# Two-layer sequence kernel: the feed-forward's first norms move in front of a branch, into a pool of their own

## The chip, the cores and the metric

One core of one Trainium2 chip. Its engines work side by side, each through its own list of instructions in order: TensorE (PE, with its weight loads PEld), VectorE (DVE), ScalarE (ACT), GpSimd (POOL), and SyncE (SP), which here only starts DMAs. The metric is the device time of one execution in microseconds, the median of several runs. Matrices are in 32-bit floats.

## The reference, cut to what matters

The kernel takes 4096 tokens of 256 features through two layers of two parts each, every part behind a layer norm and added back to its input:

```
x = x + attn0(norm(x))   # fast-weight memory with two decays
x = x + ffn0(norm(x))    # 8 experts, the best 2 of them for each token, hidden size 1024
x = x + attn1(norm(x))   # RWKV: time mix with a recurrence, then channel mix
x = x + ffn1(norm(x))    # five ternary weight matrices, three hidden layers of 1024
```

The change touches the last line's norm, and the order of work between the second, third and fourth line:

```
h = silu(x @ w1.T * s1) * (x @ w2.T * s2)
h = gelu(h @ h1.T * sh1);  h = gelu(h @ h2.T * sh2);  y = h @ w3.T * s3
```

## The kernel before

**Stages.** The first stage does attn0 and routes the tokens; its SBUF pools are then closed (`ctx_a.close()`, line 1240). What follows is in two blocks with a branch between them.

- In front of the branch, the experts of ffn0 run over slots of 256 tokens (`experts`, line 1307): 31 slots that are surely needed. attn1 works on chunks of 256 tokens (`mixing`, line 1466); chunk n needs only finished expert rows, so its steps are mixed in between the experts' steps. The same block checks the feed-forward's weights in 22 parts (`ff_check`, line 1261): a DMA brings a part into the one buffer `fft`, and three DVE instructions (`differences`: round, compare, reduce) count in `odd` whether any weight would change by rounding. `ff_flag` (line 1282) puts the 22 counts together with a transpose on PE.
- The branch (`other_slots`, line 1422; profile line 1425) tests on every engine whether a 32nd and further slots are in use. With these inputs none is: each engine takes the arm without work, where it only raises the semaphores that the other arm would have raised.
- Behind the branch, the rest of attn1 is mixed with ffn1 (`ff_split`, line 1912), which works on pairs of chunks. Each 512-token operand is split into a rounded part `hi` and a rest `lo`, so that each product is two matmuls with float32r operands. The weights come in 22 parts per pair, with DMAs that POOL starts (`fetch`, line 1978; the tile `part` has four buffers).

**The order** is written out by hand. A step is put into a `Plan` with a time and a rank, and `run` emits the steps in order of time, then rank, then entry. In the front block the unit is one step of an expert slot, 16 to a slot: for slot s, `up` at 16s to 16s+7, `down` (of a slot that isn't the last) at 16s+24 to 16s+31, the copy `xgT` (`keep`, line 1352) at 16s-7, the two `y` additions (`add`, line 1378) at 16s+28 and 16s+32, the `ys_d` store on POOL (line 1384) at 16s+32. Part q of the weight check is loaded at 12q and counted at 12q+9.5. attn1 has a time of its own, 22 units to a chunk (`TURN`, `WHEN`, line 1454): a step of chunk n is due at 22n plus its entry in `WHEN`, for example `sides` 32, `flip_c` and `keep_c` 54, the third `share` 33; the result of chunk n (from 1 on) is there at 22n+74. `among` (line 1301) turns such a time into a front time, from 208 on. All steps before `CUT` go into the front block, the others (`later`) behind the branch.

**The norm of ffn1** belongs to `pair`. For each chunk, `moments` (line 1940) takes mean and variance on DVE, `roots` (line 1948, through `root_of`, line 1440) adds epsilon on DVE and takes the power -0.5 on POOL, `norm` (line 1952) scales on DVE into `xf`, `flip` (line 1961) transposes on PE into `xfT`, and `keep` (line 1971) splits into `xf_p_hi` (ACT) and `xf_p_lo` (DVE). `first` (line 1997) is the first product, profile tile `pf`. For chunks 1 and 2, the first pair, the steps are due at 98 to 101.5 and 120 to 123.5, times before or about at the cut; being part of `ff_split` they come at the head of the block behind the branch.

**Memory.** Pools on the left side of SBUF are stacked: the weights and pools of attn1 (`rw`, `cc`, `c1`, `c2`), later `d2` of ff_split. The experts' pools (`me`, `mw`, `mt`) are on the right and are closed behind the branch (`moe_stack.close()`, line 2171). `d2` is then opened over the gap and over their bytes. A pool opened without an option waits as a whole: the first instruction of each engine that touches it waits for everything that was closed before. `mw` and `mt` have `reuse_waits="tile"`: there each tile waits only for what lay in its own bytes.

Of the kernel before, what the change touches and what calls it, by code (L numbers as in the profile page):

```python
# [8 lines left out]
F32 = mybir.dt.float32  # L9
# [3 lines left out]
ALU = mybir.AluOpType  # L13
AX = mybir.AxisListType

P = 128
S = 4096
D = 256
# [32 lines left out]
def mk_seq_kernel(ctx: ExitStack, tc: tile.TileContext, a: dict, out: bass.AP):  # L51
    nc = tc.nc
# [15 lines left out]
    ident = const.tile([P, P], F32, name="ident")  # L68
# [40 lines left out]
    for o, nm in ((0, "WkT"), (DS, "WqT"), (2 * DS, "WvT"), (3 * DS, "pwT")):  # L109
        n = a[nm].shape[1]  # L110
        nc.sync.dma_start(
            out=w_pj[:, :, o : o + n], in_=a[nm].rearrange("(c p) n -> p c n", p=P)
# [3 lines left out]
    for o, nm in ((0, "WvT"), (DS, "ir_w1T")):  # L116
        nc.sync.dma_start(
            out=w_vi[:, :, o : o + DS], in_=a[nm].rearrange("(c p) n -> p c n", p=P)
        )
    irb = ac.tile([P, 1], F32, name="irb")  # L120
    o, _ = _COLS["ir_b1"]
# [18 lines left out]
    def bcast(ap, shape):  # L140
        return ap.to_broadcast(shape)

    class Plan:
# [5 lines left out]
        def at(self, time, rank, step):  # L149
            self.steps.append((time, rank, len(self.steps), step))  # L150
# [7 lines left out]
    MIX, OUT, FEED, REST = range(4)  # L158
# [59 lines left out]
    with tc.tile_pool(name="pow", bufs=1) as tmp:  # L218
        shift1 = tmp.tile([P, P + 1], F32, name="shift1")
        nc.gpsimd.affine_select(  # L220
            out=shift1, in_=ones, pattern=[[1, P + 1]], compare_op=ALU.is_equal, fill=0.0,
# [31 lines left out]
        out=before, in_=ones[:, : NE * NE].rearrange("p (i j) -> p i j", i=NE),  # L253
# [7 lines left out]
    for q in range(2):  # L261
        t = ac.tile([P, NT, 4, DS], F32, name=f"kq{q}")
# [3 lines left out]
    for q in range(3):  # L266
        t = ac.tile([P, P], F32, name=f"h{q}")
# [12 lines left out]
    for r in range(2 * NE * S // (8 * P)):  # L280
        d, r = (xe_d, ys_d)[r * 8 * P // (NE * S)], r % (NE * S // (8 * P))
        nc.sync.dma_start(
            out=d[r * 8 * P : (r + 1) * 8 * P, :].rearrange("(p r) d -> p r d", r=8),
            in_=bcast(zero.unsqueeze(1), [P, 8, D]),
# [37 lines left out]
        out=earlier, in_=ones[:, :P], pattern=[[1, P]], compare_op=ALU.is_gt, fill=0.0,  # L322
# [20 lines left out]
    def moments(b, z, key, i):  # L343
        if i == 0:
            z["st"] = a2.tile([P, NT, 6], F32, tag=f"{key}_st", name=f"{key}_st_{b}")
            z["mv"] = a2.tile([P, NT, 2], F32, tag=f"{key}_mv", name=f"{key}_mv_{b}")
        nc.vector.bn_stats(out=z["st"][:, i, :], in_=X[b][:, i, :])
        nc.vector.bn_aggr(out=z["mv"][:, i, :], in_=z["st"][:, i, :])
# [838 lines left out]
    def table_end():  # L1187
# [28 lines left out]
    at = (  # L1216
        ((END - 25, END - 17), (END - 17, END - 5)), ((END - 5, END + 3), (END + 3, END + 12.5)),
        ((END + 13, END + 21), (END + 21, END + 29)), ((END + 29, END + 37), (END + 37, END + 45)),
    )
# [22 lines left out]
    ctx_r = ExitStack()  # L1242
# [18 lines left out]
    def ff_check(plan, time, q):  # L1261
        nm, src, j, kc, n = FFP[q]
        z = {}

        def load():
            z["t"] = mt.tile([P, kc, n], F32, tag="fft", name=f"fft_{q}", bufs=1)
            nc.sync.dma_start(
                out=z["t"], in_=a[src][j * P : (j + kc) * P, :].rearrange("(c p) n -> p c n", p=P)
            )

        def differences():
            r = mt.tile([P, kc, n], F32R, tag="ffr", name=f"ffr_{q}", bufs=1)
            nc.vector.tensor_copy(r, z["t"])
            nc.vector.tensor_tensor(z["t"], z["t"], r.bitcast(F32), ALU.not_equal)
            nc.vector.tensor_reduce(
                odd[:, q : q + 1], z["t"].rearrange("p c n -> p (c n)"), AX.X, ALU.max
            )

        for k, step in ((0, load), (9.5, differences)):
            plan.at(time + k, REST, step)  # L1280

    def ff_flag():
# [10 lines left out]


    SLOT = 2 * NF
    CUT = 120

    NSURE = 2 * S // SL + 3 - NFULL
    AMONG = ((0, 0.0), (6, 8.3), (7, 9.5), (8, 12.5), (12, 24.5), (22, 3.0 * SLOT))
# [108 lines left out]
    def first_slots():  # L1408
        plan = experts(range(NSURE), NSURE - 1)
        for k, (w, nm) in enumerate(((w_tm, "W_tm"), (w_cm, "W_cm"), (w_cp, "W_cp"))):  # L1410
            plan.at(
                40 + 20 * k, REST,
                lambda w=w, nm=nm: nc.sync.dma_start(
                    out=w, in_=a[nm].rearrange("(c p) n -> p c n", p=P)
                ),
            )
        for q in range(len(FFP)):
            ff_check(plan, 12 * q, q)
        plan.at(12 * len(FFP) + 4, REST, ff_flag)
        return plan  # L1420
# [14 lines left out]
    NI = TC // P  # L1435
# [4 lines left out]
    def root_of(rs, var):  # L1440
        nc.vector.tensor_scalar(rs, var, LN_EPS, None, ALU.add)
        nc.gpsimd.tensor_tensor(rs, rs, mhalf[:, 0, :], ALU.pow)
# [5 lines left out]
    def tokens(d, n):  # L1448
        return d[n * TC : (n + 1) * TC, :].rearrange("(i p) d -> p i d", p=P)
# [5 lines left out]
        load=2, gathers=(-2, -1, 0, 1), combine=12, moments=13, roots=13, norm_a=14, norm_i=14,  # L1455
# [453 lines left out]

    def ff_split(own, plan):

        d2 = own.enter_context(tc.tile_pool(name="d2", bufs=2))
        at = plan.at
        TP = 2 * TC
        banks = [0]
# [1 line left out]
        def psf(shape, name):  # L1919
            banks[0] += 1  # L1920
            if banks[0] % 4:
                return psa(shape, name)
            return ps.tile(shape, F32, tag="p", name=name, bufs=1)
# [12 lines left out]
        def pair(p, two, base):  # L1936

            z = {"part": {}}

            def moments(g):  # L1940
                n, x, _ = two[g]
                st = d2.tile([P, NI, 6], F32, tag="st", name=f"ln5_st_{n}", bufs=1)
                mv = z["mv"] = d2.tile([P, NI, 2], F32, tag="mv", name=f"ln5_mv_{n}", bufs=1)
                for i in range(NI):
                    nc.vector.bn_stats(out=st[:, i, :], in_=x()[:, i, :])
                    nc.vector.bn_aggr(out=mv[:, i, :], in_=st[:, i, :])

            def roots(g):
                z["rs"] = d2.tile([P, NI], F32, tag="rs", name=f"ln5_rs_{two[g][0]}", bufs=1)
                root_of(z["rs"], z["mv"][:, :, 1])  # L1950

            def norm(g):
                n, x, _ = two[g]
                z["xn"] = d2.tile([P, NI, D], F32, tag="xn", name=f"xf_{n}", bufs=1)
                for i in range(NI):
                    nc.vector.tensor_scalar(
                        z["xn"][:, i, :], x()[:, i, :], z["mv"][:, i, 0:1], z["rs"][:, i : i + 1],
                        ALU.subtract, ALU.mult,
                    )

            def flip(g):
                z["pt"] = psf([P, 2, TC], f"xfT_{two[g][0]}")
                for c in range(2):
                    for i in range(NI):
                        nc.tensor.transpose(  # L1965
                            z["pt"][:, c, i * P : (i + 1) * P],
                            z["xn"][:, i, c * P : (c + 1) * P], ident,
                        )

            def keep(g):  # L1970
# [93 lines left out]
                nc.sync.dma_start(out=tokens(out, two[g][0]), in_=z["ot", g])  # L2064

            for g in range(2):
                for t, rank, step in (
                    (1, REST, moments), (1, REST, roots), (2, REST, norm), (4.5, MIX, flip),
                    (4.5, REST, keep),
                ):  # L2070
                    at(two[g][2] + t, rank, lambda step=step, g=g: step(g))
                for t, rank, step in ((44, REST, again), (49, REST, store)):
                    at(base + t + 2 * g, rank, lambda step=step, g=g: step(g))
            for j in range(NF):
# [3 lines left out]
            for l, src in ((0, "h0"), (1, "sh1")):  # L2078
                t = base + 14 + 2 * NF * l
# [79 lines left out]

    front = Plan()  # L2160
    chunks = mixing(ctx_r, front)
    front.steps.sort(key=lambda s: s[:3])
    later = [s for s in front.steps if s[0] >= CUT]
    both = first_slots()
# [7 lines left out]
    with ExitStack() as own:  # L2172
        plan = Plan(later)
        pair = ff_split(own, plan)
        chunks = chunks[1:] + chunks[:1]
        for n, x, time in chunks:
            plan.at(time, REST, lambda n=n, x=x: nc.sync.dma_start(out=tokens(x2_d, n), in_=x()))
        for p in range(NC // 2):
            two = chunks[2 * p : 2 * p + 2]
            pair(p, two, two[1][2])  # L2180
        with tc.manual_schedule():
            plan.run()
# [92 lines left out]
```

## Time and profile before

| what | value |
|---|---|
| runs | 2042.1, 2046.39, 2045.76 us; median 2045.76 |
| the profiled execution | 2045.78 us |
| its span, first to last instruction | 2044.3 us |
| PE, PEld busy | 1951.9 us (95%), 1656.1 us (81%) |
| DVE, ACT, POOL busy | 1244.0 us (61%), 1016.1 us (50%), 437.8 us (21%) |
| mean granted TensorE clock | 0.983 |
| DMA | 314.86 MB, mean 154 GB/s |

How to read the lines: the profile follows one execution. Its row by slices cuts the span in 40 parts and gives the busy tenths of an engine in each. The chain of work is followed back from the last instruction to what released it, step by step. A row of the timeline has the start in us, the duration, engine, line, operation, the tiles written and read, the shape, a count, and in brackets how long the engine was idle before it and what ended that. A `q` behind an engine's name is its queue: branches and waits that aren't counted as busy. By stage, each column is one engine's busy us with its number of instructions; behind them stand the granted clock, the DMA share and GB/s.

### The profile page before, as it was taken

To read this page: it belongs to the slowest core of one execution; us is meant where nothing else is said; L and a number is where in the kernel's file an instruction comes from. 1 tells how busy PE (TensorE), PEld (TensorE's weight loads), DVE (VectorE), ACT (ScalarE), POOL (GpSimd) and SP (SyncE) were. 2 spreads that over 40 slices of the span, in tenths; PEclk is the share of its full clock that TensorE was granted. 3 is DMA by queue.
4 is the path that set the end of the run, shared out by engine and by line. 5 is a ranking of instruction groups with operands and counts; after the bars stand their busy time and mean duration, and the time that the engine had idled before them with its cause. 6 is when DMAs were issued, how large, how long until landed. Compare 5 with 4: busy or idle time off the path is not lost. (4 is left out here: it accounts for less than half of the span.)

```text
span 2044.3 us, 27834 instructions
## 1 busy us (share of the span) xinstructions
PE 1951.9 (95%) x9879; PEld 1656.1 (81%) x9879; DVE 1244.0 (61%) x3013; ACT 1016.1 (50%) x1918; POOL 437.8 (21%) x523
## 2 busy tenths in 40 slices
PE   6999999988899999999997999999999999999998
PEld 4888777777677888888886888888888888888887
DVE  4677888876333435564635768687676876754342
ACT  3665555433222223454534656577565675744342
POOL 1000222222300012121112223232323322122121
PEclk8999999988999999999998999999999999999999
DMA  9999300023477677554433555555565555555585
GB/s 316 342 343 343 110 32 32 32 84 102 168 260 266 227 252 249 178 178 150 147 124 84 109 118 119 114 135 103 113 135 103 134 111 118 109 114 119 102 179 105
DMA packets 328856, 314.86 MB, mean 154 GB/s; under 512 B 18177, under 2 KB 308609, under 8 KB 328705
## 3 DMA queue, kind: packets, MB, share of 16 engines
q1 hardware_dynamic: 158624, 187.61, 28.1%
q0 software_dynamic: 170080, 125.33, 27.9%
q8 instruction: 83, 1.36, 0.3%
q14 instruction: 69, 0.56, 0.1%
HBM read 215.64 MB, written 97.26 MB: 153 GB/s over the span
## 5 line engine op out<-in xcount | busy, mean ns | idle before, releaser
L1086 ACT ACTIVATE hT<-peh,b 128x256 f32<-128x256 f32 x248 | 115.6, 473 | 291.3 <-PE peh L1359 285.8
L1359 PE MATMUL peh<-xgT,w 128*128 128x256 f32 x992 | 229.2, 385 | 8.6 <-DVE y L1381 6.5
L1373 PE MATMUL peo<-w,hT 128*128 128x256 f32 x992 | 224.9, 379 | 0.0
L1359 PEld LDWEIGHTS peh<-xgT,w 128*128 128x128 f32 x992 | 189.2, 193 | 38.7 <-DVE y L1381 9.4
L1932 PE MATMUL psh<-h_hi,part 128*128 128x512 f32 x512 | 211.1, 412 | 0.0
L1932 PE MATMUL psh<-sh_hi,part 128*128 128x512 f32 x512 | 209.2, 409 | 0.0
L1373 PEld LDWEIGHTS peo<-w,hT 128*128 128x128 f32 x992 | 186.7, 190 | 24.4
L2045 DVE TENSOR_TENSOR sh_lo<-hf_sh,sh_hi 128x512 fp32r<-128x512 f32 x128 | 88.3, 690 | 186.3 <-ACT sh_hi L2044 186.3
L1932 PE MATMUL psh<-h_lo,part 128*128 128x512 f32 x512 | 200.5, 392 | 0.0
L1932 PE MATMUL psh<-sh_lo,part 128*128 128x512 f32 x512 | 200.2, 391 | 0.0
L2039 ACT ACTIVATE hf_sh<-psh,vec 128x512 f32<-128x512 f32 x128 | 87.8, 686 | 225.8 <-PE psh L1932 225.4
L619 PE MATMUL pf<-LY,LT 128*128 128x256 f32 x640 | 181.1, 386 | 3.4 <-DVE LY L645 2.2
L645 DVE TENSOR_TENSOR LY<-pf,LY 128x256 f32<-128x256 f32 x192 | 79.0, 417 | 77.4 <-ACT LY L641 50.2
L619 PEld LDWEIGHTS pf<-LY,LT 128*128 128x128 f32 x640 | 106.2, 191 | 22.2 <-issue 6.3
L1827 PE MATMUL pcm<-xcT,w_cm 128*128 128x256 f32 x512 | 120.9, 379 | 0.0
L1860 PE MATMUL pcp<-k,w_cp 128*128 128x256 f32 x512 | 120.9, 379 | 0.0
L612 ACT COPY LT<-pt 128x256 f32<-128x256 f32 x192 | 71.4, 372 | 87.7 <-PE pt L608 79.2
L1932 PEld LDWEIGHTS psh<-h_lo,part 128*128 128x128 f32 x512 | 96.3, 188 | 20.1 <-DVE h_lo L2045 0.4
L1932 PEld LDWEIGHTS psh<-sh_lo,part 128*128 128x128 f32 x512 | 96.3, 188 | 19.7
L1932 PEld LDWEIGHTS psh<-sh_hi,part 128*128 128x128 f32 x512 | 96.3, 188 | 19.5
L1932 PEld LDWEIGHTS psh<-h_hi,part 128*128 128x128 f32 x512 | 96.3, 188 | 19.4
L1860 PEld LDWEIGHTS pcp<-k,w_cp 128*128 128x128 f32 x512 | 97.0, 189 | 14.9
(421 smaller groups left out, 4186.4 us busy)
## 6 DMA issues: line engine op xcount, KB each, us to landing
w<-in_w_dram SPq DMA_DIRECT2D x62, 1024.0 KB
xe_d<-zero SPq DMA_DIRECT2D x32, 1024.0 KB
ys_d<-zero SPq DMA_DIRECT2D x32, 1024.0 KB
part<-in_h1T_dram POOLq DMA_DIRECT2D x64, 512.0 KB
part<-in_h2T_dram POOLq DMA_DIRECT2D x64, 512.0 KB
w_f<-in_w_dram SPq DMA_DIRECT2D x8, 1024.0 KB
part<-in_w1T_dram POOLq DMA_DIRECT2D x32, 256.0 KB
part<-in_w2T_dram POOLq DMA_DIRECT2D x32, 256.0 KB
```

The costliest lines, as they stand in the source:

```text
L612: nc.scalar.copy(y["LT"], y["pt"])
L619: nc.tensor.matmul(p[:, f].rearrange("p g t -> p (g t)"), LT[:, f, :], L[:, f].rearrange("p g t -> p (g t)"), start=True, stop=True,)
L645: nc.vector.tensor_tensor(N[:, :, 1, :], p[:, :, 1, :], L[:, :, 1, :], ALU.add)
L1086: nc.scalar.activation(out, x, AF.Gelu_apprx_tanh, bias=bias)
L1359: nc.tensor.matmul(z["ph", h], z["w1"][:, c, h * P : (h + 1) * P], z["xT"][:, c, :], start=(c == 0), stop=(c == 1),)
L1373: nc.tensor.matmul(z["px"], z["hT"][:, h, i * P : (i + 1) * P], z["w2"][:, h, :], start=(h == 0), stop=(h == NF - 1),)
L1827: nc.tensor.matmul(pk[:, u, :], w_cm[:, c, j * P : (j + 1) * P], z["xnT"][:, c, :], start=(c == 0), stop=(c == 1),)
L1860: nc.tensor.matmul(z["pv"][:, c, :], w_cp[:, j, c * P : (c + 1) * P], z["k2"][:, g, h, u, :], start=(half == 0 and q == 0), stop=(half == ...
L1932: nc.tensor.matmul(pp, w, x[u][:, k, :], start=(k == 0 and u == 0), stop=(k == kk - 1 and u == 1))
L2039: nc.scalar.activation(h, z[nm, j], AF.Gelu, scale=col(nm, j))
L2045: nc.vector.tensor_tensor(lo[:, j, :], h, hi[:, j, :].bitcast(F32), ALU.subtract)
```

## The change

Three things change.

1. `ff_norm`, a new function, does what `moments`, `roots` and `norm` did, with tiles from a new pool `cf` that is opened in front of the branch, on top of `c2`. The steps go into the front plan at the same times as before (`time` is 22n+75, and the steps lie 1, 1 and 2 behind it). `xf` has two buffers instead of one. `pair` now gets the normalized tile in place of the chunk, and its `flip` is due at the old time or at `CUT`, whichever is later.
2. `CUT` goes from 120 to 121.5. So the norms of chunks 1 and 2 (98, 99, 120, 121) are in front of the branch, and with them the steps of attn1 that are due from 120 up to 121.5: `flip_c` and `keep_c` of chunk 3, `sides` and the third `share` of chunk 4. `d2` gets `reuse_waits="tile"`.
3. `differences` of the weight check are due 11 units after their load instead of 9.5.

```
-        for k, step in ((0, load), (9.5, differences)):
+        for k, step in ((0, load), (11, differences)):
...
-    CUT = 120
+    CUT = 121.5
...
+    def ff_norm(cf, at, n, x, time):
+        z = {}
+        def moments():
+            st = cf.tile([P, NI, 6], F32, tag="st", name=f"ln5_st_{n}")
+            mv = z["mv"] = cf.tile([P, NI, 2], F32, tag="mv", name=f"ln5_mv_{n}")
+            for i in range(NI):
+                nc.vector.bn_stats(out=st[:, i, :], in_=x()[:, i, :])
+                nc.vector.bn_aggr(out=mv[:, i, :], in_=st[:, i, :])
+        def roots():
+            z["rs"] = cf.tile([P, NI], F32, tag="rs", name=f"ln5_rs_{n}")
+            root_of(z["rs"], z["mv"][:, :, 1])
+        def norm():
+            z["xn"] = cf.tile([P, NI, D], F32, tag="xn", name=f"xf_{n}", bufs=2)
+            for i in range(NI):
+                nc.vector.tensor_scalar(
+                    z["xn"][:, i, :], x()[:, i, :], z["mv"][:, i, 0:1], z["rs"][:, i : i + 1],
+                    ALU.subtract, ALU.mult,
+                )
+        for t, step in ((1, moments), (1, roots), (2, norm)):
+            at(time + t, REST, step)
+        return lambda: z["xn"]
...
-        d2 = own.enter_context(tc.tile_pool(name="d2", bufs=2))
+        d2 = own.enter_context(tc.tile_pool(name="d2", bufs=2, reuse_waits="tile"))
...
-                            z["xn"][:, i, c * P : (c + 1) * P], ident,
+                            two[g][1]()[:, i, c * P : (c + 1) * P], ident,
...
-                for t, rank, step in (
-                    (1, REST, moments), (1, REST, roots), (2, REST, norm), (4.5, MIX, flip),
-                    (4.5, REST, keep),
-                ):
-                    at(two[g][2] + t, rank, lambda step=step, g=g: step(g))
+                for rank, step in ((MIX, flip), (REST, keep)):
+                    at(max(two[g][2] + 4.5, CUT), rank, lambda step=step, g=g: step(g))
...
     chunks = mixing(ctx_r, front)
+    chunks = chunks[1:] + chunks[:1]
+    cf = ctx_r.enter_context(tc.tile_pool(name="cf", bufs=1))
+    chunks = [(n, x, time, ff_norm(cf, front.at, n, x, time)) for n, x, time in chunks]
...
-            two = chunks[2 * p : 2 * p + 2]
+            two = [(n, xn, time) for n, _, time, xn in chunks[2 * p : 2 * p + 2]]
```

The three inner functions `moments`, `roots` and `norm` of `pair` are removed with it.

More of the change, by code (lines that the diff above doesn't have):

```diff
@@ L1938, in pair @@
             z = {"part": {}}
[L1940 to L1959, printed above, removed]
             def flip(g):
@@ L2174, in mk_seq_kernel @@
         pair = ff_split(own, plan)
-        chunks = chunks[1:] + chunks[:1]
-        for n, x, time in chunks:
+        for n, x, time, _ in chunks:
             plan.at(time, REST, lambda n=n, x=x: nc.sync.dma_start(out=tokens(x2_d, n), in_=x()))
         for p in range(NC // 2):
-            two = chunks[2 * p : 2 * p + 2]
+            two = [(n, xn, time) for n, _, time, xn in chunks[2 * p : 2 * p + 2]]
             pair(p, two, two[1][2])
```

## The prediction

> **What bounds the kernel.** I read the page first. TensorE (PE) is busy 95% of the 2044.3 us span, and the row by slices has few dips:
>
> ```profile
> PE   6999999988899999999997999999999999999998
> ...
> PE 41%; ACT 3%; DVE 1%; another core or an unknown queue 0%; issue 0%; POOL 0%; DVEq 0%; POOLq 0%; ACTq 0%
> ```
>
> The chain that ended last is 41% PE and begins at 1086.65 us with a wait on something unnamed; from 1106 us to the end it is nearly all matmuls. So what shortens PE's idle time before 1106 us shortens the kernel. PE's idle by stage (columns: window, its length, then busy us of PE, its weight load, DVE, ACT, POOL, granted clock, DMA):
>
> ```profile
> 1040.00:1080.00 40.00, 39.97 (x192) 34.88 (x191) 13.05 (x32) 14.83 (x28) 3.42 (x5) 1.00 0.33 109
> 1080.00:1110.00 30.00, 18.65 (x81) 15.24 (x80) 14.69 (x40) 9.22 (x13) 9.21 (x13) 0.83 0.29 79
> 1110.00:1130.00 20.00, 20.00 (x95) 16.87 (x94) 18.15 (x31) 14.65 (x28) 7.54 (x8) 1.00 0.66 136
> ```
>
> PE is full on both sides of the branch and loses 11.4 us at it. The timeline there:
>
> ```profile
> 1085.76 0.42 DVE L1381 TENSOR_TENSOR y<-peo,b 128x256 f32<-128x256 f32 x1 [3.03 <-PE peo L1373]
> 1086.49 0.73 POOL L1384 DMA_DIRECT2D ys_d<-y  x1 [6.18 <-DVE y L1381]
> 1092.29 0.43 DVE L1945 BATCH_NORM_STATS2 ln_st<-xt 128x6 f32<-128x256 f32 x1 [6.10 <-DMA yg<-ys_d,placei]
> ...
> 1093.89 0.71 POOL L1442 TENSOR_TENSOR ln_rs<-ln_rs,mhalf 128x2 f32<-128x2 f32 x1 [6.68 <-DVE ln_rs L1441]
> 1094.57 0.73 POOL L1995 DMA_DIRECT2D part<-in_w1T_dram  x1
> ...
> 1095.26 1.09 PE L1965 MATMUL xfT<-ident,xf 128*128 128x128 f32 x4 [9.53 <-DVE xf L1956]
> ...
> 1106.37 0.50 PE L1932 MATMUL pf<-xf_p_lo,part 128*128 128x512 f32 x1 [1.80 <-DVE xf_p_lo L1975]
> ```
>
> PE's last expert matmul ends at 1085.72. Nothing runs until DVE's first norm at 1092.29; DVE, POOL, DVE, then PE follow in single file. What held DVE is shown by the branch's line:
>
> ```profile
> L1425 PEldq COMPARE_BRANCH x1: 3731/3731/3731, 1082.3 to 1082.3; - x1
> L1425 PEldq EVENT_SEMAPHORE  x1: 51/51/51, 1086.1 to 1086.1; - x1
> ...
> L1425 DVEq EVENT_SEMAPHORE  x1: 21/21/21, 1086.6 to 1086.6; - x1
> ...
> L1425 POOLq INC_SWDGE_SEM  x1: 1527/1527/1527, 1089.9 to 1089.9; - x1
> ```
>
> In the empty arm each engine raises its counters to what the untaken arms would have left. PE is through at 1086.16, DVE at 1086.65. POOL first waits for the last expert store (its semaphore completes at 1089.62), then raises the DMA counters, until 1091.43. DVE, ACT, PE and POOL each stand at nine waits on all these counters at the head of line 1945, 1974, 1965 or 1442, all in the first instruction that touches pool `d2`. At 0.1 us each these run from 1091.42 to 1092.29 on DVE.
>
> **Part 1, waits tile by tile.** Whether a tile of `d2` still waits for POOL's counters is decided by its bytes. In the compiled program of before, `c2` ends at byte 114,824 of a partition and `mt` begins at 137,952. The new pool takes about 4.2 KB of that gap, so `d2` starts near 119,070: the split tiles `xf_p_hi`/`lo` end near 127,270 and the first `part` buffer near 131,360. All lie in the gap, over first-stage memory released hundreds of us earlier. Tiles over `xg` and `y` (second `part` buffer, hidden layer) still wait for 1091.43, but POOL can't issue before that anyway and the hidden layer is written after 1097. I take the wait as gone for PE, ACT and DVE. PE's first transposes need DVE's arm (1086.65, the PSUM bank) and one 0.1 us step: start 1086.75 instead of 1095.26. Bounds: 1086.16 (PE's own arm) and 1092.35 (nine waits remain; rival 1).
>
> **Part 2, norms in front.** Per chunk: statistics, sum and scale 1.4 us DVE, 0.71 us POOL, 0.76 us DVE. They go before the branch. Cover: DVE is busy 13.05 of 40 us at 1040:1080 and idles 6.84 us before the last `xgT`; the power stands on POOL behind a store already issued (1052.46) and ahead of one that waits 12.6 us more. Cost there: nothing; without cover up to the round trip, 2.2 us per chunk. What else the new cut pulls in front: `sides` of chunk 4 (1.4 us DVE, same cover); `keep_c` and the last `share` (1.0 and 0.9 us ACT between gelus of 0.47 us each 0.86 us, three PSUM banks: nothing to 1.9 us; I take nothing, the gap of 0.39 per gelu being nearest); and `flip_c`, four transposes at 0.11 us steps on a full PE: **+0.44 us**. SP's next `xt` load (1095.42) no longer waits for a norm behind the branch and can't collide with the weights.
>
> **PE from 1086.75**, at full-clock steps (0.44 for four transposes, 1.73 for eight 256-wide matmuls): xfT 1087.2, pkvr 1088.9, pcm 1090.65, xfT 1091.1, pcm 1092.8. DVE meanwhile: lo at 1088.8, combine 1.65 to 1090.5, mix 0.87 to 1091.4, statistics and roots 1.43 to 1092.8, second lo 0.69 to 1093.5 (ACT's hi is done by 1092). Next late are the weights. POOL, without the powers, issues part 0 at 1091.5 and 1092.2; in before, three of the first four landed 3.2 to 3.5 us after issue (one 5.6, beside the `xt` load): 1094.9 and 1095.6. So the first 8 matmuls of `first(0)` (0.93 us per 4) run 1094.9 to 1096.75. In before the matmul after them began at 1108.09. **Gain 11.3 us.** DVE reaches the end of `xa` at 1096.65 (before 1109.35), in time for the transposes at 1098.5; after that PE is as full as at 1110:1130, so the shift stays.
>
> **Part 3, counts 1.5 units later.** DVE is in order, so a later time matters only where another DVE step lies in between. Expert steps lie at 9, 12 and 16 of each 16 units, the counts at 9.5, 5.5, 1.5, 13.5 and now at 11, 7, 3, 15: nothing between. Mixing steps begin at 208; only the last count (261.5 to 263) passes any: `maxima`, `mix(1)`, `steps` of chunk 0 (261.5, 262.9). There:
>
> ```profile
> 807.70 0.69 DVE L1273 CAST ffr<-fft 128x1024 fp32r<-128x1024 f32 x1 [5.91 <-DMA fft<-in_w3T_dram]
> ...
> 810.89 1.39 DVE L1655 TENSOR_TENSOR_SCAN m<-vec,carry_m,kvr 128x256 f32<-128x256 f32 x2
> ...
> 817.24 0.17 DVE L1283 TENSOR_REDUCE flag<-odd 128x1 f32<-128x22 f32 x1
> ```
>
> DVE idles 5.91 us for the last weights, then does `maxima`; PE waits 2.74 us for `flag` at 817.46. Reordered, `maxima` fits into the idle, `mix` runs when pkvr ends (808.1), the count from 810.2, flag near 816.0: **1.2 us less** (bounds 0 and 2.7).
>
> **Sum:** -11.3 + 0.44 - 1.2 = -12.1. The profiled execution took 2045.78 (span 2044.3 and 1.5 around it), the median of the runs is 2045.76: **2033.7 us**. Own range 2031.3 (flag's whole 2.7 saved, weights not waited for) to 2036.5 (weights 2.2 us later, as in the 5.6 us row; ACT 0.6).
>
> The clock: it was 0.5 for 10.24 us from 1089.13, after a 3.41 us window with PE idle. A window with PE 38% busy (543.00 to 546.41) was followed by 3.41 us at half, two at 60% (812.65 to 819.47) were not. My two pauses (1.0 and 2.1 us) leave 70% and, if the second falls into one window, about 40%: a drop of 3.41 us would cost 1.7, inside the range; I leave it out, since the phase of the windows is open. [...]
>
> **Rivals.**
>
> 1. *The waits stay* (a first tile still overlaps expert memory; the option doesn't do what it says). PE starts at 1092.35 at half clock until 1099.4: transposes 0.88, pkvr 3.46, pcm to 1099.8, the rest to 1101.9, next matmul at 1103.75: 4.35 saved, in all -5.1: 2040.7. For it: the arm's counters are still raised at 1091.4; against: the byte positions. 0.12.
>
> 2. *PE pays a second jump.* Its COMPARE_BRANCH took 3.73 us, hidden under matmuls until 1086.05. If the jump out of the arm costs as much, PE starts at 1089.9 behind an idle window, at half clock to about 1092.5; the matmul after `first(0)` begins near 1100: -8.9, 2036.9. Against: at the kernel's end PE took 3.35 us into the arm, but its next instruction followed the arm's wait within 0.2 us. 0.10. [...]
>
> 3. *Slower: late counts block DVE.* If a later count stood in front of an expert add, PE would stop as at 651.12, where DVE stood at a count for weights: 4.61 us idle and 3.41 us at half clock, 6.3 in all. Five counts stand just before an add; from two more such stops the 12.1 is gone, three give +6.8: 2052.6. Against: the order on DVE doesn't change there. 0.06.
>
> 4. *Gain given back* between 1097 and 1130, where DVE is 91% busy: within 4 us of now. 0.08.
>
> Forecast 0.64. Rival 1 lies just beyond the 0.2% (4.1 us) that a measurement of this kernel can tell from no change; I leave it with faster: 0.86 faster, 0.08 same, 0.06 slower. The range 2031.3 to 2040.9 holds forecast, rivals 1 and 2.
>
> **What would show it.** Right: PE's gap at the branch about 1 us, then at most 2 us before the first `pf`; no half clock there; `part` issued just after INC_SWDGE_SEM; `flag` gap near 1.5. Wrong: a `d2` tile in the tail of expert memory, PE starting after 1091, or new gaps before `peh` between 580 and 800.

## The result, and the profile after

| what | before | after |
|---|---|---|
| median of six runs each, same chip | 2043.82 us (2040.31 to 2046.39) | 2032.71 us (2031.69 to 2036.04) |
| ratio | 1 | 0.9948 (95%: 0.9935 to 0.9962) |
| the profiled execution, its span | 2045.78, 2044.3 us | 2033.08, 2031.6 us |
| PE, DVE, ACT, POOL busy | 1951.9, 1244.0, 1016.1, 437.8 us | 1952.6, 1244.1, 1016.8, 437.5 us |
| mean granted clock | 0.983 | 0.984 |

The kernel is faster by 11.1 us by the medians; the engines do the same work. In the page of the changed kernel, the row of PE by slices (40 slices of 50.8 us) and the chain of work by engine:

```profile
PE   6999999989898999999999999999999999999998
...
PE 77%; DVE 10%; ACT 5%; DMA 5%; issue 2%; POOL 1%; SPq 0%; POOLq 0%; DVEq 0%; ACTq 0%
```

The slice with the branch is at 9 like its neighbours, where it had a 7 before. The chain no longer begins at the branch: it can be followed back through it to the experts, and 77% of it is PE. Across the branch itself it still isn't PE's: there the view leads from a store of the experts (`ys_d`, until 1087.96) to ACT's `xf_p_hi`, DVE's list and the first product at 1093.84. By stage (columns as before: window, length, busy us of PE, PEld, DVE, ACT, POOL, granted clock, DMA):

```profile
1040.00:1080.00 40.00, 39.97 (x194) 34.78 (x193) 14.00 (x36) 15.27 (x30) 4.42 (x6) 1.00 0.40 122
1080.00:1110.00 30.00, 25.96 (x123) 21.31 (x122) 19.73 (x41) 17.84 (x30) 11.39 (x14) 1.00 0.54 119
1110.00:1130.00 20.00, 20.00 (x93) 16.87 (x92) 15.13 (x26) 8.61 (x16) 4.69 (x5) 1.00 0.51 101
```

In front of the branch PE is as full as it was, with one norm's DVE and POOL work more beside it (chunk 2's, 1050.35 to 1053.34; chunk 1's is done at 988). At the branch it loses 4.0 us instead of 11.4, and the clock stays at 1. The timeline there:

```profile
1083.97 0.30 PE L1971 MATMUL xfT<-ident,xf 128*128 128x128 f32 x1 [1.07 <-DVEq L1425]
1086.06 0.49 PE L1971 MATMUL xfT<-ident,xf 128*128 128x128 f32 x3 [1.78 <-issue]
...
1088.11 1.89 PE L1827 MATMUL pcm<-xcT,w_cm 128*128 128x256 f32 x8
1088.17 0.59 ACT L1980 CAST xf_p_hi<-xfT 128x512 fp32r<-128x512 f32 x1 [18.57 <-DMA yg<-ys_d,placei]
1088.59 0.73 POOL L2001 DMA_DIRECT2D part<-in_w1T_dram  x1 [4.19 <-DMA yg<-ys_d,placei]
...
1088.79 0.69 DVE L1981 TENSOR_TENSOR xf_p_lo<-xfT,xf_p_hi 128x512 fp32r<-128x512 f32 x1 [5.42 <-ACT xf_p_hi L1980]
...
1093.84 0.50 PE L1959 MATMUL pf<-xf_p_lo,part 128*128 128x512 f32 x1 [0.75 <-DVE xf_p_lo L1981]
...
1095.58 1.89 PE L1827 MATMUL pcm<-xcT,w_cm 128*128 128x256 f32 x8
```

PE starts 1.07 us behind its last expert matmul (1082.90), as forecast. Two things are not as forecast. PE stops again after one transpose, for 1.78 us, with no releaser but "issue". And ACT's `xf_p_hi`, whose source was ready at 1086.56, begins at 1088.17, just when POOL's raising of the DMA counters is over; the DMA that the row names had long been over (its last issue was at 1031.10). DVE stands behind ACT, and 5 us later PE stands behind DVE's second `xf_p_lo`. PE's branch instruction took 3.3 us, under matmuls, where before had 3.7, and POOL's counter instruction took as long as before (count, shortest, median and longest duration in ns, then first and last start in us):

```profile
L1425 PEldq COMPARE_BRANCH x1: 3297/3297/3297, 1079.5 to 1079.5; - x1
...
L1425 POOLq INC_SWDGE_SEM  x1: 1527/1527/1527, 1086.5 to 1086.5; - x1
```

The pause before the transpose of `flag` is 1.42 us; it was 2.74:

```profile
814.19 0.27 PE L1285 MATMUL pfl<-ident,flag 128*1 128x128 f32 x1 [1.42 <-DVE flag L1283]
```

### How far single pieces can be read

Device times of one program move by some 6 us from run to run (2040.31 to 2046.39 for before) and by 8 us from chip to chip (medians of before from 2042.99 to 2050.88). Most of this lies in front of `flag`: the first expert slot begins between 556.6 and 567.2 us in the thirteen profiled executions of this study. Behind that, pieces are reproducible to 0.1 us at equal clock, but for a second pause of PE behind the branch, which moves by up to 0.9 us between executions. So I read three of them from every trace, one profiled execution of each kernel: PE's pause before `flag`; the time from the transpose of `flag` to the end of the last expert matmul; and the **branch time**, from there to the first matmul behind the first `first` step (1082.90 to 1095.58 above). From that matmul to PE's end it was 927.8 to 927.9 us in eleven of the thirteen, whatever stood in front, and 928.2 and 928.6 in e2 and e6, where a halved clock reached past it: what is gained at the branch is kept.

| kernel | device time, median | ratio to before (95%) | pause before flag | flag to last expert | branch time |
|---|---|---|---|---|---|
| before | 2043.82 | 1 | 2.74 | 268.27 | 22.37 |
| changed | 2032.71 | 0.9948 (0.9935 to 0.9962) | 1.42 | 268.71 | 12.68 |
| e1 option alone | 2041.18 | 0.9990 (0.9981 to 1.0000) | 2.71 | 268.25 | 19.81 |
| e2 without the option | 2032.32 | 0.9941 (0.9928 to 0.9955) | 1.42 | 268.73 | 14.40 |
| e3 counts alone | 2041.33 | 0.9993 (0.9984 to 1.0002) | 1.42 | 268.26 | 22.30 |
| e4 split first | 2031.43 | 0.9938 (0.9924 to 0.9951) | 1.42 | 268.74 | 11.40 |
| e5 changed, no branch | 2035.24 | 0.9922 (0.9905 to 0.9938) | 1.42 | 268.73 | 7.87 |
| e6 CUT 120 | 2044.98 | 0.9965 (0.9950 to 0.9979) | 1.42 | 268.51 | 17.48 |
| e7 split first, loads later | 2029.53 | 0.9892 (0.9875 to 0.9908) | 1.42 | 268.74 | 14.47 |
| e8 before, no branch | 2047.98 | 0.9986 (0.9975 to 0.9997) | 2.96 | 269.70 | 19.80 |
| e9 e8 and the option | 2043.04 | 0.9963 (0.9949 to 0.9976) | 3.08 | 271.12 | 15.61 |
| e10 changed, again | 2040.39 | 0.9949 (0.9932 to 0.9966) | 1.42 | 268.74 | 12.68 |
| e11 as e7, again | 2029.98 | 0.9902 (0.9886 to 0.9918) | 1.42 | 268.73 | 11.22 |

e1 to e4 ran on one chip (before: 2042.99), e5 to e8 on a second (2050.88), e9 to e11 on a third (2049.67). Ratios, not medians, are compared across them.

### The profile page after: what moved, and what is told of

The parts are those of the page before. It is cut to its first block, busy times and chain, and to the rows that moved or that the text cites. A ratio compares the mean times of both kernels' runs of the same rounds, so it can differ in the third digit from the quotient of the medians.

```text
span 2031.6 us, 27809 instructions
## 1 busy us (share of the span) xinstructions
PE 1952.6 (96%) x9879; PEld 1656.4 (82%) x9879; DVE 1244.1 (61%) x3013; ACT 1016.8 (50%) x1918; POOL 437.5 (22%) x523
## 4 chain that ended last, share of the span: by engine, by line
PE 77%; DVE 10%; ACT 5%; DMA 5%; issue 2%; POOL 1%; SPq 0%; POOLq 0%; DVEq 0%; ACTq 0%
PE psh L1959 20%; PE peh L1359 8%; PE peo L1373 7%; PE pf L1959 6%; PE pcp L1860 5%; PE pcm L1827 5%; PE pf L619 5%; PE pkvr L1612 4%; PE pf L2028 2%; DMA ys_d<-y 2%; DMA fft<-in_h1T_dram 1%; PE pt L608 1%; PE pp L402 1%; PE pf L624 1%; PE px L821 1%
## 5 line engine op out<-in xcount | busy, mean ns | idle before, releaser
L1359 PEld LDWEIGHTS peh<-xgT,w 128*128 128x128 f32 x992 | 189.8, 194 | 40.2 <-DVE y L1381 10.4
## 6 DMA issues: line engine op xcount, KB each, us to landing
xe_d<-zero SPq DMA_DIRECT2D x32, 1024.0 KB, 11.1
ys_d<-zero SPq DMA_DIRECT2D x32, 1024.0 KB, 11.4
```

Source lines behind the costliest of these rows:

```text
L1359: nc.tensor.matmul(z["ph", h], z["w1"][:, c, h * P : (h + 1) * P], z["xT"][:, c, :], start=(c == 0), stop=(c == 1),)
```

## The experiments

### e1: the option alone

```
-        d2 = own.enter_context(tc.tile_pool(name="d2", bufs=2))
+        d2 = own.enter_context(tc.tile_pool(name="d2", bufs=2, reuse_waits="tile"))
```

> The kernel before with one edit: the pool d2 waits tile by tile. The norms of the first pair stay behind the branch. Measure: the time from the end of the last expert matmul (peo) to the first matmul behind the first `first` step (the second pcm after it); it was 22.37 us in the kernel before (1085.72 to 1108.09) and 12.68 in the changed one (1082.90 to 1095.58). Theory A (the power on POOL holds the norm): DVE begins the statistics right behind its own arm, but POOL is in its arm until about 5.7 us after the last matmul, so the power, the scaling and the first transposes come only about 2.1 us earlier than before; PE still idles over 7 us, then runs at half clock. Expected 20.3 us (19.8 to 20.9), device time 2 us under before. Theory B (the waits for the whole pool are the cost, as the prediction put it under part 1): most of the 9.7 us come with the option alone; expected 14 to 17 us, device time 5.5 to 8 us under before.

Measured 19.81 us, 2.56 less than before. In the timeline of this kernel, whose last expert matmul ends at 1083.80:

```profile
1084.81 0.43 DVE L1945 BATCH_NORM_STATS2 ln_st<-xt 128x6 f32<-128x256 f32 x1 [0.54 <-DVEq L1425]
...
1089.46 0.71 POOL L1442 TENSOR_TENSOR ln_rs<-ln_rs,mhalf 128x2 f32<-128x2 f32 x1 [4.17 <-DMA yg<-ys_d,placei]
```

DVE starts the statistics 0.54 us behind its last addition, 5.6 us earlier than in before (counted from the last expert matmul), and is done with them at 1086.2. Then the power waits for POOL, which is in its arm until 1089.4. The option frees DVE, and POOL's arm takes its place: theory A.

### e2: the norms in front, without the option

```
-        d2 = own.enter_context(tc.tile_pool(name="d2", bufs=2, reuse_waits="tile"))
+        d2 = own.enter_context(tc.tile_pool(name="d2", bufs=2))
```

> The changed kernel with one edit taken back: d2 waits as a whole again. The norms are in front of the branch. Theory A: the first transposes and the attn1 matmuls don't touch d2, so PE starts as in the changed kernel, 1.07 us behind the last expert matmul; ACT's and DVE's first split and POOL's first weight stand at nine waits instead of three, which costs about 0.7 us. Expected 13.3 us (13.0 to 13.8) from the last expert matmul to the matmul behind the first `first` step, against 12.68 in the changed kernel; device time 9 to 11 us under before. Theory B: without the option the waits are back: 18 us or more, device time at most 5 us under before.

Measured 14.40 us, outside the expected 13.0 to 13.8, and far from theory B's 18. PE starts after 1.07 us as in the changed kernel. ACT's first split starts 5.80 us behind the last expert matmul (5.27 there) and DVE's second ends at 11.41 (10.88): the option is worth 0.53 us once the norms are in front. The rest of the miss is the clock. The seven last of the eight matmuls of `first` came every 0.43 us instead of 0.23, which is 1.19 us. By windows (the granted clock is the third number from the end):

```profile
1088.20:1091.60 3.40, 1.49 (x6) 0.75 (x5) 3.30 (x11) 1.78 (x3) 1.84 (x3) 0.99 1.13 271
1091.60:1095.00 3.40, 3.40 (x9) 2.64 (x8) 3.40 (x8) 3.04 (x4) 3.04 (x5) 0.50 0.60 147
```

3.4 us in which PE was 44% busy were followed by 3.4 us at half clock. Without that the branch time would have been 13.2.

### e3: the counts alone

```
-        for k, step in ((0, load), (9.5, differences)):
+        for k, step in ((0, load), (11, differences)):
```

> The kernel before with the counts of the weight check 11 units behind their loads instead of 9.5, nothing else. Both theories as in the prediction: PE's pause before the transpose of `flag` goes from 2.74 us to 1.4 (it was 1.42 in the changed kernel), no other pause appears or goes; device time 1.3 us under before (0.6 to 2). Rival: the pause in the changed kernel was shorter for another reason (it is 2.7 here again), or the late counts cost elsewhere (new pauses of PE before 1080 us); then device time is that of before or more.

The pause before `flag` is 1.42 us, to 0.01 us that of the changed kernel; the other pieces are those of before (268.26; 22.30, and 950.15 us from the last expert matmul to PE's end, where before has 950.19). The device time is 1.7 us lower, with an interval that reaches to no change. The 1.32 us of the pause are the whole effect of the counts.

### e4: the first split tiles into the gap

```
+        x_first = halves("x", [P, 2, TP], "xf_p0", 1)
...
-                    z["x"] = halves("x", [P, 2, TP], f"xf_p{p}", 1)
+                    z["x"] = halves("x", [P, 2, TP], f"xf_p{p}", 1) if p else x_first
```

> The changed kernel with the first pair's split tiles xf_p_hi and xf_p_lo allocated when d2 is opened, ahead of the weight buffers. Their bytes move from 135,456 to 143,648 (over expert memory that begins at 137,952) to 119,072 to 127,264, in the gap; nothing else is changed. Theory A (the bytes made ACT and DVE wait for POOL's counters): xf_p_hi begins within 0.2 us of the end of the first transposes, about 3.7 us behind the last expert matmul (5.27 in the changed kernel), DVE's second xf_p_lo is done near 9.4 us behind it instead of 10.9, and what is late next is the second half of the first weights, 10.6 us behind it. Expected 11.6 us (11.2 to 12.1) to the matmul behind the first `first` step, against 12.68; device time about 1 us under the changed kernel. Rival: ACT and DVE were held by something else than the bytes: xf_p_hi begins 5.2 us behind the last expert matmul again and 12.7 us stay.

Measured 11.40 us. The waits are gone, as the timeline of this kernel shows (last expert matmul: 1081.09):

```profile
1085.09 0.59 ACT L1982 CAST xf_p_hi<-xfT 128x512 fp32r<-128x512 f32 x1 [17.31 <-PE xfT L1973]
...
1090.03 0.68 DVE L1983 TENSOR_TENSOR xf_p_lo<-xfT,xf_p_hi 128x512 fp32r<-128x512 f32 x1
```

`xf_p_hi` follows the transposes (done at 1085.05) and its releaser is now PE. It is 4.00 us behind the last expert matmul, not 3.7, because PE's second pause was 2.11 us this time. One part of the expectation was wrong: the weights were not late next. They landed 9.1 and 10.1 us behind the last expert matmul, and PE came to them at 9.26 and 10.47 without a pause. From 1084.56 on PE is full to within 0.2 us; what is left is its start (1.07) and its second pause (2.11).

### e5: the changed kernel without the branch

```
-    n_slots = nc.values_load(counti, min_val=0, max_val=NREST)
-    other_slots(NSURE)
```

> The changed kernel without the branch: the test for a 32nd and further slots and their work are left out (with these inputs no such slot is in use). It measures what the branch still costs in the changed kernel. Theory: without the arms there is no jump (PE's 1.78 us pause with an instruction fetch beside it goes), DVE needn't be waited for (1.07 us) and POOL needn't wait for the last expert store and raise the DMA counters (until 5.1 us behind the last expert matmul); then DVE's list alone (split, combine, mix, statistics, second split) is what is late. Expected from the end of the last expert matmul to the first matmul behind the first `first` step: 8.1 us (7.4 to 9), against 12.68 in the changed kernel; device time 4.5 us under it. Rival: the pause of PE isn't the branch's (the instruction fetch comes with any new stretch of code): it stays, and the measure is 9.5 us or more.

Measured 7.87 us. PE goes from the last expert matmul (its end: 1087.19) into the transposes and the products without a pause over 0.2 us:

```profile
1087.03 0.60 PE L1971 MATMUL xfT<-ident,xf 128*128 128x128 f32 x4
1087.46 1.89 PE L1612 MATMUL pkvr<-xiT,w_tm 128*128 128x256 f32 x8
```

So the branch still costs 4.8 us in the changed kernel, and PE's second pause is the branch's.

### e6: the cut back at 120

```
-    CUT = 121.5
+    CUT = 120
```

> The changed kernel with CUT back at 120, so that only the first chunk's norm is in front of the branch; the second chunk's statistics, power and scaling, and flip_c, keep_c, sides and the third share, are behind it again. Theory: the power of the second chunk stands on POOL behind its arm and the first weight part (issued near 5.7 us and 6.4 us behind the last expert matmul), so it runs near 7.2 us, the second transposes near 8.8 instead of 6.9, and the second xf_p_lo, which the products wait for, about 2.4 us later. Expected 15.1 us (14.3 to 17, the upper end if the clock halves in the pause) against 12.68; in front 0.44 us less (268.27 us between the transpose of flag and the last expert matmul, as in before, against 268.71); device time 2 us over the changed kernel. Rival: the second norm is covered by other work: 12.4 to 13 us, device time as the changed kernel.

Measured 17.48 us, above the expected range; the device time is 0.17% above the changed kernel's ratio, 3.5 us, with intervals that overlap. In the trace `flip_c`, `keep_c` and `sides` of these chunks stand in front of the branch in this kernel too (half of `flip_c`, and so `keep_c`, behind the last expert matmul; why, the record doesn't show), so it differs from the changed one by less than I meant: the second chunk's norm and a share. Its path was not the one that I expected either (last expert matmul: 1089.38):

```profile
1096.29 0.69 DVE L1981 TENSOR_TENSOR xf_p_lo<-xfT,xf_p_hi 128x512 fp32r<-128x512 f32 x1 [6.45 <-ACT xf_p_hi L1980]
1096.90 0.42 DVE L1920 BATCH_NORM_STATS2 ln_st<-xt 128x6 f32<-128x256 f32 x1
...
1098.42 0.70 POOL L1442 TENSOR_TENSOR ln_rs<-ln_rs,mhalf 128x2 f32<-128x2 f32 x1 [0.87 <-DVE ln_rs L1441]
```

POOL had been idle for 0.87 us when the power came. The statistics stand on DVE behind the first `xf_p_lo`, which waits for POOL's counters; statistics, power and scaling then lie on the path, 3.0 of the 4.8 us over the changed kernel. Another 1.0 us is that ACT's first split began later (6.29 us behind the last expert matmul instead of 5.27), behind POOL's counters. The last 0.8 us is clock: it was 0.5 for 3.4 us from 1094.7 and again from 1105.0, there under `first`. So both chunks' norms have to be in front.

### e7: attn1's weights loaded later, on top of e4

```
-                40 + 20 * k, REST,
+                (40, 120, 160)[k], REST,
```

> The kernel of e4_split_first with attn1's weights W_cm and W_cp loaded at 120 and 160 of the front plan instead of 60 and 80. It measures the price that the prediction put on an expert addition or copy behind a late weight count (6.3 us: PE idle and then at half clock near 650 us). Theory: that stop comes from the load of a checked part queued behind W_cp on SP's queue (its issue took 3.91 us, the data came 12 us later); with W_cm and W_cp away from it, the pause of 4.6 to 6 us before `peh` near 650 us and the half clock behind it go, and device time is about 6 us under e4_split_first (near 2025.5 us). Rival: the pause is due to the expert weights themselves, or moves to where the loads now lie: device time within 2 us of e4_split_first.

The pause near 650 us is gone: from the first `pxg` to the transpose of `flag` it took 246.48 us, where e4 took 255.74. One stop of DVE at a late weight count cost 9.3 us, then: 5.95 us of PE idle and 6.8 us at half clock. The device time is 21 us below before, by the ratios 9.4 us under e4, where 6 were expected. The branch time was 14.47 instead of 11.40 with the instructions and their order as in e4; 0.3 us of that is a longer second pause, 2.8 the clock:

```profile
1079.50:1083.00 3.50, 0.84 (x4) 0.34 (x3) 0.42 (x1) 0.00 (x0) 0.73 (x1) 0.99 0.23 77
1083.00:1089.40 6.40, 5.61 (x15) 4.57 (x15) 3.60 (x10) 3.87 (x4) 2.90 (x4) 0.50 0.29 73
```

PE's two pauses (1.06 and 2.39 us) lay in one stretch of 3.5 us here, in which it was 24% busy; 6.8 us at half clock followed (1082.95 to 1089.78), of which the second row shows 6.4. In that row the eight matmuls of `pkvr` took 3.41 us from the first to the next group (1084.39 to 1087.80); in the changed kernel, at full clock, they took 1.73 (1086.38 to 1088.11).

### e8 and e9: the kernel before without the branch, and with the option

e8 takes the same two lines out of the kernel before as e5; e9 adds the edit of e1 to it.

> The kernel before without the branch (the work for slots beyond the 31st is left out; with these inputs there is none). It tells how much of the 9.7 us gained at the branch were the branch's own and how much is the norms' path DVE, POOL, DVE, PE behind the last expert matmul. Theory: without arms the statistics follow the last expert addition, the power starts at once on POOL, and PE's first transposes come 3.5 us behind the last expert matmul at full clock; expected 13.3 us (12.4 to 14.5) to the first matmul behind the first `first` step, against 22.37 with the branch, so that the norms in front would be worth 5 us even without a branch (8.1 expected there); device time 9 us under before. Rival: the wait for the whole pool holds it also without the branch: 16 us or more.

> The kernel before without the branch (as in e8_before_no_branch, it leaves out the work for slots beyond the 31st, of which these inputs have none), and with d2 waiting tile by tile. Theory: in e8 the statistics stood 3.53 us until the last expert store had landed, since the pool d2 waits as a whole for all expert memory, that store's source too; with waits by tile the statistics start behind the last expert addition, the power follows on POOL at once, and PE's first transposes come 3.5 us behind the last expert matmul instead of 6.86; the rest of the way is DVE's list as before (12.4 to 12.9 us from the first transposes to the end of `first` in e1 and e8). Expected 15.9 us (15.3 to 16.6) against 19.80 in e8; device time 3.5 us under e8. Rival: POOL's own list (the store, then the power) holds the norm: 18 us or more.

e8: 19.80 us, not 13.3; the rival was right. Without the branch the kernel before gains only 2.57 us, and its device time is 2.9 us lower, not 9. e9: 15.61 us, 4.2 less, in the expected range; 3.8 of it is PE's earlier start (3.04 us behind the last expert matmul instead of 6.86), and half clock followed in both, for 6.8 us in e8 and 3.4 in e9. What held the norms in e8, and what follows in e9:

```profile
1093.12 0.43 DVE L1945 BATCH_NORM_STATS2 ln_st<-xt 128x6 f32<-128x256 f32 x1 [3.53 <-DMA ys_d<-y]
```

```profile
1090.63 0.42 DVE L1945 BATCH_NORM_STATS2 ln_st<-xt 128x6 f32<-128x256 f32 x1
...
1092.09 0.71 POOL L1442 TENSOR_TENSOR ln_rs<-ln_rs,mhalf 128x2 f32<-128x2 f32 x1 [0.34 <-DVE ln_rs L1441]
```

With a pool that waits as a whole, the first statistics wait for the last expert store to land, since its source lay in expert memory; with waits by tile they follow the last addition (e9's ended at 1090.71). (The longer way from `flag` to the last expert matmul in both is half clock behind a `flag` pause of about 3 us: in e8 the clock was 0.50 for 3.4 us from 818.9, in e9 for 6.8 us from 818.1.)

### e10 and e11: the changed kernel and e7 on one chip

No edit: e10 is the changed kernel, e11 the kernel of e7.

> The changed kernel once more, beside the next one and on its chip. Nothing is changed: it shows how far the time at the branch moves from run to run with the same program. Expected: 268.7 us from the transpose of flag to the last expert matmul and 1.42 us before the transpose, as in every kernel with the change; from the last expert matmul to the matmul behind the first `first` step 12.7 us if the granted clock stays at 1 there, 14 to 16 if it halves in the pauses (as it did in e2 and e7); device time 11 us under before (9.5 to 13).

> The kernel of e7_loads_later once more, beside the changed kernel and on its chip: the first split tiles in the gap, and W_cm and W_cp loaded at 120 and 160. Expected: no pause near 650 us, so 9 us less than the changed kernel between the first expert slot and flag (246.5 us from the first pxg to the transpose of flag, against 255), and 1.1 us less at the branch at equal clock; device time 9 to 10.5 us under the changed kernel. Rival: the gain of e7 was that chip's: 2 to 6 us.

e10 repeats the changed kernel to 0.03 us in all three pieces, 12.68 us at the branch among them, with the clock at 1. Its device time is 9.3 us under before by the medians, just short of the expected 9.5 to 13. e11 has 11.22 us there, now at full clock, and 245.50 us up to `flag`. Its median is 10.4 us under that of the changed kernel beside it, and its ratio to before, 0.9902 (0.9886 to 0.9918), agrees with the 0.9892 of the same program in e7. No other version comes as low.

## Why the prediction was right, and which step of it failed

The time came out 1.0 us under the forecast of 2033.7. Part of that is luck: the gain summed from the pieces below was 1.5 us smaller than forecast, and the median from which it was counted (2045.76, three runs) was 1.9 us above that of six runs.

| term | forecast | measured |
|---|---|---|
| part 3, pause before `flag` | -1.2 | -1.32 (changed, and e3 alone) |
| part 2, norms and `flip_c` in front | +0.44 | +0.44 (268.27 to 268.71) |
| branch | -11.3 | -9.69 (22.37 to 12.68; again in e10) |
| sum | -12.1 | -10.6 |

The two profiled executions differ by 12.7 us. The other 2 us are the front's movement: the first expert slot began 4.13 us earlier, and from there to the transpose of `flag` it took 0.87 us more, although the pause in front of it was 1.32 us shorter.

**Parts 2 and 3** were right in mechanism and size. DVE's, ACT's and POOL's added work in front cost nothing; four transposes on a full PE cost their 0.44 us; the reordered last count gave its pause and nothing else.

**The step that failed is in part 1:** "the split tiles `xf_p_hi`/`lo` end near 127,270 and the first `part` buffer near 131,360. All lie in the gap". I had only moved the old layout up by the size of the new pool. In the compiled programs, a pool's tiles lie in the order in which they are first asked for. Before, the split of chunk 1 was due at 101.5, ahead of the first weight fetch. With the new `CUT` it is due at 121.5, behind the fetches at 119.3 and 121.3. So the four weight buffers take 119,072 to 135,456, and the split tiles 135,456 to 143,648, over `odd` and the expert tiles from 137,952 on. The wait was gone for PE only. ACT and DVE still stood at POOL's counters: the first `xf_p_lo` was done 6.58 us behind the last expert matmul, where I had 3.1, and with DVE's list behind it the second at 10.88, where I had 7.8. DVE, not the weights, was late next. The bytes are those of the compiled program, which no trace shows; e4 tests them: it moves the two tiles, and 1.28 us come back. Of the signs that the prediction named for being wrong, this one was there: tiles of `d2` over expert memory.

**What the prediction gave the wrong weight.** It put the whole gain under the waits. e1 and e2 divide it: the option alone gives 2.56 us, the norms in front alone 7.97 (9.2 at full clock), both 9.69. The waits on the whole pool and POOL's arm held the same path one behind the other. With the option alone, the power still stands behind POOL's arm. With the norms in front, PE needs neither. e8 and e9 show the same without the branch: there the pool's wait costs 4.2 us by the last store. And most of the gain isn't the branch's. Without it the way from e8 (19.80) to e5 (7.87) is 11.93 us, 4.19 by the option (e9) and 7.74 by what the changed kernel does in front; with it the changed kernel gained 9.69. What was saved is mostly the norms' own way over DVE, POOL, DVE and PE, which no longer stands behind the last expert matmul. The 5 us that e8's expectation gave the norms in front without a branch were too few.

**The rivals.** Rival 1 did not happen to PE, but its mechanism, a first tile over expert memory, happened to ACT and DVE. Its start of PE, 6.6 us behind the last expert matmul, rested on a wait that PE no longer meets once the norms are in front: the first transposes touch no tile of `d2`, and in e2, where the pool waits as a whole, PE starts after 1.07 us too. Rival 2 was half right: PE does stop a second time, for 1.52 to 2.42 us in the seven traces with the branch and the norms in front of it, not 3.73. In the changed kernel a record of the instruction queue lies beside it, by DMA queue in 1083.30 to 1084.70:

```profile
q8 instruction: 1, 0.02, 4.9%
```

These 16 KB began at 1083.48, 0.5 us behind PE's arm, and were there at 1084.58 (4.9% of 16 engines in 1.4 us is 1.1 us of one); PE went on at 1086.06. The kernel before has such a record at 1086.77, inside its longer wait. The changed kernel has another at 1087.29, when PE is in `pkvr` (1086.38 to 1088.11), and PE doesn't stop for it. So a record alone is no pause. That the branch makes the pause is shown by e5, which has no pause over 0.2 us there; that PE waits in it for these 16 KB is a guess, which no run shows, and no view names the engine that a record belongs to. In the changed kernel the pause cost nothing, since ACT's split stood at POOL's counters longer than that (until 1088.17); in e4 it is the largest piece left (2.11 us). Rival 3 did not occur: DVE's order changed nowhere but at the last count (e3). Its price of 6.3 us came from one stop of 4.61 us with 3.4 us at half clock. In the changed kernel this stop took 5.79 us and in e4 5.95, with 6.8 at half clock in both, and e4's cost 9.3 (against e7). Rival 4 did not occur: from the branch time's end to PE's end it is 927.8 us in before and 927.9 us in the changed kernel.

**The clock** was left out with the remark that a drop was open. At the branch it did not fall in either profiled execution of the changed kernel; it fell in e2 (1.19 us), in e6 (0.8) and in e7 (2.8, the same program as e11). The size that I gave a drop, 1.7 us, lies between. The same program met a drop in e7 and none in e11, where the clock was 1.00 from 1079 to 1091; why is not shown. In before the stretches at half clock begin at 491.80, 546.41, 563.48, 655.64 and 1089.13 us, whole multiples of 3.41 us apart: these are the windows of the prediction. The drop in e2 came behind 3.4 us in which PE was 44% busy.

**What stays open:** what in POOL's arm takes the 1.53 us of its counter instruction, and whether PE's second pause has to do with the 16 KB beside it at all, and, if so, how much of the 1.48 us between their arrival (1084.58) and PE's next instruction (1086.06) belongs to it.

## What to carry to other kernels

Before a step is moved in front of a barrier, list every queue on its path: here DVE's wait on the pool, POOL's arm and PE's order lay one behind the other, and taking away the first alone gave a quarter of the gain (2.56 of 9.69 us, e1). When a due time changes, look again at the order in which a pool's tiles are first asked for, since it decides their bytes, and with waits by tile the bytes decide who waits (1.28 us in e4). Where a run moves more than the change, measure the change between two fixed events in the trace, and look at the granted clock before calling a difference an effect.

## What the runs showed of the hardware

- Half clock followed 3.4 us with PE 44% busy (e2), 3.5 us with PE 24% busy (e7) and 3.4 us with PE 36% and, later, 47% busy (e6: 1091.32 to 1094.73, 1101.56 to 1104.97), and lasted 3.4, 6.8, 3.4 and 3.4 us. Pauses of 1.07 and 1.78 us (changed kernel) and of 1.06 and 1.52 us (e10) at the same place passed without it.
- Behind the branch of the changed kernel a record of 16 KB in the instruction queue took 1.10 us (1083.48 to 1084.58), and PE went on 1.48 us after its end. In seven traces with the branch PE paused there for 1.52 to 2.42 us; without the branch (e5) it has no pause over 0.2 us.
- Where one DVE step waited for a late load, PE stopped for 5.95 us and its clock was at 0.50 for 6.8 (e4, from 649.2): 9.3 us, most of what the whole change gained (11.1), and gone by loading two weights later (e7, e11).
